# The first tile of a fused RWKV and feed-forward block: one difference for the shares, other mixings, a second norm without its mean

## The chip, the cores and the metric

The kernel runs on one core of one Trainium2 chip. The metric is the device time of one execution in microseconds (us); a profile of one such execution shows every instruction with its engine: PE (TensorE matmul), PEld (its weight loads), DVE (VectorE), ACT (ScalarE), POOL (GpSimd) and SP (SyncE, here only a DMA queue).

## The reference

Input x has 2 sequences of 4096 steps with 256 features, all in float32. The block is x + attention(norm(x)), then x + feed-forward(norm(x)). The norm has no scale or offset.

```python
def _layernorm(x, axis=-1, eps=1e-05):
    m = jnp.mean(x, axis=axis, keepdims=True)
    v = jnp.var(x, axis=axis, keepdims=True)
    return (x - m) / jnp.sqrt(v + eps)

# attention: x_prev is x one step earlier, zero at the start of a sequence
xk = x * time_mix_k + x_prev * (1.0 - time_mix_k)      # likewise xv, xr
k = jnp.einsum('btd,ed->bte', xk, W_k)                 # likewise v, and r through a sigmoid
# one step of the recurrence, p and q its state:
new_p = jnp.maximum(p, u + k_t)
scale_old = jnp.exp(jnp.maximum(p - new_p, NEG_CLAMP))
scale_cur = jnp.exp(jnp.maximum(u + k_t - new_p, NEG_CLAMP))
wkv_t = (scale_old * q + scale_cur * v_t) / (scale_old + scale_cur + EPS)
new_p2 = jnp.maximum(p + w, k_t)
q2 = jnp.exp(jnp.maximum(p + w - new_p2, NEG_CLAMP)) * q + jnp.exp(jnp.maximum(k_t - new_p2, NEG_CLAMP)) * v_t
# output: einsum of r * wkv with W_o

# feed-forward, with ternary weights and a scale for each output
h = jax.nn.silu(_tlin(x, w1_w, w1_s)) * _tlin(x, w2_w, w2_s)
h = jax.nn.gelu(_tlin(h, h1_w, h1_s), approximate=False)
h = jax.nn.gelu(_tlin(h, h2_w, h2_s), approximate=False)
return _tlin(h, w3_w, w3_s)
```

The two weights of `wkv_t` are a sigmoid of the difference u + k - p and of its negative; the kernel computes them so, and calls them shares.

## The kernel before

Features lie on the 128 partitions, in two heads (halves of the 256 features, index `h` or `c`); time lies along the free axis in 16 tiles of `TS` = 512 steps, of which 8 make a sequence. `halves` are the two halves of a tile in time. The feed-forward products run on TensorE in a rounded type, each value as a high and a low part (`split_product`, L186 and L187; `split`, L193 and L194). The attention products, the means and the norms of the first tile are full float32.

From the second tile on, the attention of tile i + 1 (`attention`, with `wkv` for a head) and the first norm of tile i + 2 (`normalise`, through `layernorm` and `total`) are generators whose pieces are placed between the pieces of the feed-forward of tile i (`ffn`); the loop at the end of `split_block` says at which step of `ffn` a piece is emitted. Their sums over features go to GpSimd as an all-reduce over the partitions (L207, with the sum of the two heads before it at L205).

The first tile has nothing to hide behind, so `first_tile` is written out by hand: every operation of it goes through `on` (line 358 in the profile, whatever the operation), which queues it behind the last one on the same engine. An operation can be emitted inside `behind(engine)` or `in_turn()`. Both rest on `tc.issue_after(ins)`, which orders only the instructions of the block that are on the engine of `ins`, behind `ins` in that engine's queue; it adds no wait between engines. Where such an order is missing, the scheduler may issue an instruction as soon as it thinks it ready, as it does with the copies of the carried state in `wkv` (L252, L253).

In order, the first tile does this. The means come from products with a constant matrix (`mean_w`). `first_layernorm` subtracts them, squares on ACT, adds the squares of the two heads on DVE, sums them over the features with one-column products (`var`), takes the root on ACT and the reciprocal on DVE, spreads it over the partitions with products (`rstd`) and multiplies. `keep_warm` fills PE's waits with products that nobody reads (`unread`).

The token mixing is folded into the weights of key and value (`scale`, tiles `ws`: a weight scaled by the mix and by its complement, the second applied to x one step earlier), which makes 4 products for each head; for the receptance the mixed input is built on ACT and added on GpSimd (tiles `mx`), which makes 2. `keys` are projected first, head 0 in two halves; then the values `v`, then the receptances `r`.

`differences` scans the running maximum (`lm`) and takes two differences for each head: key against the decayed state, into `sc`, and key plus `u` against the state, into `so`. `scales` makes the decay factors with Exp, two sigmoids make the shares, `state` scans the numerator (`num`), `result` multiplies and adds, and `y` is the result times r. Then come the output products (`ps_o`), the residual add into `x_sb`, again means and norm, and the rounding into `x2_hi` and `x2_lo`, with which the feed-forward of the first tile begins (`pa`, `pb`).

`load_table` evaluates a function on one column into `root` ahead of its need, so that ACT loads its table early; a small all-reduce on `root` does the same for GpSimd.

Of the kernel before, what the change touches and what calls it, by code (L numbers as in the profile page):

```python
# [9 lines left out]
F32 = mybir.dt.float32  # L10
# [56 lines left out]
def split_block(ctx, tc, flags, x, vecs, w_attn, w1, w2, h1, h2, w3, out):  # L67
# [35 lines left out]
    small = const.tile([P, 2], F32, name="small")  # L103
# [4 lines left out]
    for m, queue in enumerate((nc.scalar, nc.sync, nc.sync)):  # L108
        queue.dma_start(out=wa_sb[:, m], in_=w_attn[:, m])
# [31 lines left out]
    vector.tensor_scalar(unmix, vec[:, 0 : 3 * ND], -1.0, 1.0, ALU.mult, ALU.add)  # L141

# [59 lines left out]
    def total(a, b, tag):  # L202

        both = one.tile([P, TS], F32, tag=tag, name="both")
        marks["both"] = vector.tensor_tensor(both, a, b, ALU.add)  # L205
        everywhere = one.tile([P, TS], F32, tag="total", name="total")
        marks["sum"] = nc.gpsimd.partition_all_reduce(everywhere, both, channels=P, reduce_op=ReduceOp.add)  # L207
        return everywhere

    def layernorm(src, new_xc, tag, spread=False):  # L210


        mean = total(src[:, 0, :], src[:, 1, :], tag)
# [24 lines left out]
    def wkv(h, k, v, r, y, first):  # L238
# [9 lines left out]
        if first:  # L248
            vector.memset(lm[:, 0:1], LOG_ZERO)
            vector.memset(num[:, 0:1], 0.0)  # L250
        else:
            vector.tensor_copy(lm[:, 0:1], log_max[:, h : h + 1])  # L252
            vector.tensor_copy(num[:, 0:1], numer[:, h : h + 1])  # L253
# [33 lines left out]
    def normalise(i):  # L287
# [15 lines left out]
        yield from layernorm(x_sb, new_xn, "rstd1", spread=True)  # L303
# [3 lines left out]
    def attention(i):  # L307

        first = tiles[i][1] == 0
# [16 lines left out]
        for h in range(ND):  # L326
# [8 lines left out]
            yield from wkv(h, *kvr, y, first)  # L335
# [44 lines left out]
    def first_layernorm(src, xc, means):  # L380
# [4 lines left out]
        for mean, p in zip(means, halves):  # L385
            for h in range(ND):
                add(xc[:, h, p], src[:, h, p], mean, ALU.subtract)
            activation(sq[:, :, p], xc[:, :, p], AF.Square)
        varis = []
        for p in halves:  # L390
            add(sq[:, 0, p], sq[:, 0, p], sq[:, 1, p])
            var = ps_ffn.tile([P, TS // 2 // P], F32, tag="pf", name="var")
            for b in range(TS // 2 // P):
                t = slice(p.start + b * P, p.start + (b + 1) * P)
                matmul(var[:, b : b + 1], sq[:, 0, t], mean_w[:, 0:1], start=True, stop=True)
# [14 lines left out]
        for rstd, p in zip(spread, halves):  # L410
            for h in range(ND):
                add(xc[:, h, p], xc[:, h, p], rstd, ALU.mult)
            yield

    def first_tile(second):

        x_sb = loaded.pop(0)
        xn = wide.tile([P, ND, TS], F32, tag="wide", name="xn0")
# [23 lines left out]
        norm = first_layernorm(x_sb, xn, means)  # L442
# [3 lines left out]
        scaled = [[hid.tile([P, ND, D], F32, tag=tag, name="ws") for tag in ("hi", "lo")] for m in range(2)]  # L446
# [5 lines left out]

        next(norm)
# [8 lines left out]
        keep_warm(unread, 3, 2 * P)  # L462
        scale(0, (1, 1), (0, 1))
        scale(1, (0, 0), (1, 0), (1, 1), (0, 1))
# [3 lines left out]
        mx, then = (wide.tile([P, ND, TS], F32, tag="wide", name="mx") for _ in range(2))  # L468
        for c in range(ND):
            j = 2 * ND + c  # L470
            activation(mx[:, c, :], xn[:, c, :], AF.Copy, scale=vec[:, j : j + 1])
            activation(then[:, c, 1:], xn[:, c, : TS - 1], AF.Copy, scale=unmix[:, j : j + 1])
            on("gpsimd", "tensor_tensor", mx[:, c, 1:], mx[:, c, 1:], then[:, c, 1:], ALU.add)
        load_table(AF.Exp)
        on("gpsimd", "tensor_copy", prev, xn[:, :, TS - 1 :])

        on("gpsimd", "partition_all_reduce", root, eps, channels=P, reduce_op=ReduceOp.add)

        def project(m, h, kind, p=whole):
# [3 lines left out]
            if m == 2:  # L483
                for c in range(ND):
                    matmul(ps, wa_sb[:, 2, c, block], mx[:, c, :], start=c == 0, stop=c == ND - 1)
# [3 lines left out]
            shifted = slice(p.start + skip - 1, p.stop - 1)  # L489
            matmul(ps, now[:, 0, :], xn[:, 0, p], start=True, stop=False)  # L490
# [6 lines left out]
        keys = [[(project(0, 0, attn, p), p) for p in halves], [(project(0, 1, attn), whole)]]  # L497
        v = [project(1, h, ffn) for h in range(ND)]
        r = [project(2, h, ffn) for h in range(ND)]

        def differences(h):
            w, u = col(DECAY, h), col(FIRST, h)
            for k, p in keys[h]:
                t, after = lm[h][:, p], lm[h][:, p.start + 1 : p.stop + 1]
# [3 lines left out]
                on("vector", "scalar_tensor_tensor", so[h][1][:, p], k, u, t, ALU.add, ALU.subtract)  # L508
            on("vector", "tensor_scalar", sc[h][0], sc[h][1], NEG_CLAMP, 0.0, ALU.max, ALU.min)
            on("gpsimd", "tensor_copy", log_max[:, h : h + 1], lm[h][:, TS:])  # L510

        def scales(h):
            activation(sc[h][0], sc[h][0], AF.Exp)
            activation(sc[h][1], sc[h][1], AF.Relu)
            activation(sc[h][1], sc[h][1], AF.Exp, scale=-1.0)


        def state(h):
            on("vector", "scalar_tensor_tensor", sc[h][1], sc[h][1], MIN_SCALE, v[h], ALU.max, ALU.mult)
            on("vector", "tensor_tensor_scan", num[h][:, 1:], sc[h][0], sc[h][1], num[h][:, 0:1], ALU.mult, ALU.add)  # L520
# [440 lines left out]
```

## Time and profile before

| | us |
|---|---|
| median of 3 runs | 1541.54 (1541.45 to 1542.15) |
| the profiled execution, own time | 1540.95 |
| span of its instructions | 1539.4 |
| first feed-forward product starts | 39.16 |
| PE busy up to there | 36.61 |
| PE busy over the span | 1529.8 |

The profile has a page (busy times, chain of work that ended last, groups of instructions) and answers to questions on the trace (chain in order of time, timeline by engine, busy time in given stretches). Times count from the start of the span. In a line of the timeline stand start, length, engine, line, operation, the tiles written and read, and in brackets the idle time of the engine before it and what ended that. In a line of the windows stand the stretch and its length, then the busy time and the number of instructions of PE, PEld, DVE, ACT and POOL, then the granted clock of PE, the share of the DMA engines and GB/s. A float32 product shows as two records.

### The profile page before, as it was taken

The page shows a single profiled execution, that of the slowest core. Times are in us where ns is not written, and L with a number is a line of the kernel's source. Part 1 is how long each engine was busy: PE and PEld are TensorE (multiplying, and loading weights), DVE is VectorE, ACT ScalarE, POOL GpSimd, SP SyncE. Part 2 cuts the span into 40 slices and gives each one's busy share as a digit, 9 for nine tenths or more (in the row PEclk, how much of TensorE's full clock was granted, in tenths as well). Part 3 has the DMA queues.
Part 4 walks back from the last instruction along what each step waited for, and adds up shares of the span by engine and source line. Part 5 has one row for each costly group of instructions (what it writes and reads, how often), then busy time and mean ns, then how long its engine had stood idle before and what let it go on. Part 6 is the DMA issues. An engine that isn't in the chain of part 4 may idle for free.

```text
span 1539.4 us, 16523 instructions
## 1 busy us (share of the span) xinstructions
PE 1529.8 (99%) x6260; PEld 1172.8 (76%) x6260; DVE 1069.8 (69%) x1598; ACT 1047.3 (68%) x1348; POOL 240.5 (16%) x118
## 2 busy tenths in 40 slices
PE   9999999999999999999999999999999999999998
PEld 6778787777877778777787777877777787777886
DVE  7886676866768677785777768677686777855531
ACT  6685957759587595866858668595775858656542
POOL 4131021110211101112011121101111021100100
PEclk9999999999999999999999999999999999999999
DMA  7612030220302103031130311203122030210302
GB/s 274 137 55 89 14 118 33 82 69 14 134 18 96 55 26 133 7 110 42 45 113 14 117 35 59 93 10 120 35 77 74 14 130 21 96 41 28 117 9 83
DMA packets 39702, 109.16 MB, mean 71 GB/s; under 512 B 3712, under 2 KB 12672, under 8 KB 39104
## 3 DMA queue, kind: packets, MB, share of 16 engines
q1 hardware_dynamic: 25760, 79.86, 15.8%
q0 software_dynamic: 13296, 27.53, 5.7%
q8 instruction: 51, 0.84, 0.2%
q10 hardware_dynamic: 560, 0.66, 0.1%
q14 instruction: 35, 0.29, 0.1%
HBM read 99.64 MB, written 12.58 MB: 73 GB/s over the span
## 4 chain that ended last, share of the span: by engine, by line
PE 98%; DVE 1%; ACT 1%; issue 0%; DVEq 0%; ACTq 0%
PE ph L186 30%; PE ph L187 30%; PE pa L186 4%; PE pb L186 4%; PE po L187 4%; PE po L186 4%; PE pa L187 4%; PE pb L187 4%; PE ps_k L179 3%; PE ps_o L179 3%; PE ps_r L179 3%; PE ps_v L179 3%; PE ps_k L358 0%; PE unread L358 0%; DVE scale L358 0%; PE ps_v L358 0%
## 5 line engine op out<-in xcount | busy, mean ns | idle before, releaser
L186 PE MATMUL ph<-hi,h_sb 128*128 128x512 f32 x2048 | 815.7, 399 | 0.2 <-ACT hi L193 0.2
L187 PE MATMUL ph<-lo,h_sb 128*128 128x512 f32 x2048 | 811.5, 397 | 0.0
L186 PEld LDWEIGHTS ph<-hi,h_sb 128*128 128x128 f32 x2048 | 384.6, 188 | 98.5 <-issue 18.2
L187 PEld LDWEIGHTS ph<-lo,h_sb 128*128 128x128 f32 x2048 | 384.5, 188 | 96.9 <-issue 15.3
L207 POOL PARTITION_ALL_REDUCE total<-both x60 | 205.1, 3419 | 857.6 <-DVE both L205 442.7
L615 DVE TENSOR_TENSOR lo<-full,hi 128x512 fp32r<-128x512 f32 x256 | 197.2, 773 | 140.0 <-ACT full L614 137.1
L612 ACT ACTIVATE hi<-ph,vec 128x512 fp32r<-128x512 f32 x256 | 175.6, 686 | 125.7 <-PE ph L187 124.6
L596 ACT ACTIVATE gated<-pa,vec 128x512 f32<-128x512 f32 x128 | 87.4, 683 | 139.0 <-PE pa L187 137.2
L614 ACT ACTIVATE full<-ph,vec 128x512 f32<-128x512 f32 x256 | 175.3, 685 | 0.3
L597 DVE SCALAR_TENSOR_TENSOR gated<-pb,vec,gated 128x512 f32<-128x512 f32 x128 | 95.9, 749 | 70.9 <-PE pb L187 66.6
L612 ACT ACT_TABLE_LOAD x103 | 132.1, 1283 | 1.8
L231 DVE RECIPROCAL rstd<-rstd 128x256 f32<-128x256 f32 x60 | 102.8, 1731 | 2.1 <-ACT rstd L227 2.1
L193 ACT ACTIVATE hi<-gated 128x512 fp32r<-128x512 f32 x128 | 80.4, 628 | 33.8 <-DVE gated L597 33.5
L186 PE MATMUL pa<-x_hi,w_sb 128*128 128x512 f32 x256 | 101.9, 398 | 0.1
L186 PE MATMUL pb<-x_hi,w_sb 128*128 128x512 f32 x256 | 101.8, 398 | 0.0
L187 PE MATMUL pb<-x_lo,w_sb 128*128 128x512 f32 x256 | 100.5, 392 | 0.0
L187 PE MATMUL pa<-x_lo,w_sb 128*128 128x512 f32 x256 | 100.4, 392 | 0.0
L194 DVE TENSOR_TENSOR lo<-gated,hi 128x512 fp32r<-128x512 f32 x128 | 96.3, 760 | 4.8
L187 PE MATMUL po<-lo,w_sb 128*128 128x512 f32 x256 | 99.6, 389 | 0.0
L186 PE MATMUL po<-hi,w_sb 128*128 128x512 f32 x256 | 99.6, 389 | 0.0
L621 DVE SCALAR_TENSOR_TENSOR x_sb<-po,vec,x_sb 128x512 f32<-128x512 f32 x32 | 24.0, 751 | 72.1 <-PE po L187 72.1
L262 DVE TENSOR_TENSOR_SCAN lm<-vec,lm,ps_k 128x512 f32<-128x512 f32 x30 | 38.4, 1279 | 40.7 <-PE ps_k L179 40.7
(145 smaller groups left out, 1741.3 us busy)
## 6 DMA issues: line engine op xcount, KB each, us to landing
h_sb<-h_hbm SPq DMA_DIRECT2D x128, 512.0 KB, 3.2
raw<-in_h SPq DMA_DIRECT2D x32, 256.0 KB, 2.7
x_sb<-in_x POOLq DMA_DIRECT2D x15, 512.0 KB, 4.1
out<-x_sb POOLq DMA_DIRECT2D x15, 512.0 KB, 3.2
h_sb<-in_h POOLq DMA_DIRECT2D x1, 4096.0 KB, 18.7
h_hbm<-in_h POOLq DMA_DIRECT2D x8, 512.0 KB, 8.6
w_sb<-in_w POOLq DMA_DIRECT2D x3, 1024.0 KB, 9.6
raw<-in_w SPq DMA_DIRECT2D x12, 256.0 KB, 2.5
```

The lines of the kernel that those rows point to most:

```text
L179: tensor.matmul(psum, weights(c), src[c], start=c == 0, stop=c == n - 1)
L186: tensor.matmul(psum, weights(c), hi, start=c == 0, stop=False)
L187: tensor.matmul(psum, weights(c), lo, start=False, stop=c == n - 1)
L193: marks["rounded"] = scalar.activation(hi, full, AF.Copy)
L194: marks["rest"] = vector.tensor_tensor(lo, full, hi.bitcast(F32), ALU.subtract)
L207: marks["sum"] = nc.gpsimd.partition_all_reduce(everywhere, both, channels=P, reduce_op=ReduceOp.add)
L231: vector.reciprocal(rstd[:, p], rstd[:, p])
L596: scalar.activation(full, pa, AF.Silu, scale=col(S1, f))
L597: vector.scalar_tensor_tensor(full, pb, col(S2, f), full, ALU.mult, ALU.mult)
L612: scalar.activation(hi, ps, AF.Gelu, scale=col(scales, f))
L614: marks["rounded"] = scalar.activation(full, ps, AF.Gelu, scale=col(scales, f))
L615: marks["rest"] = vector.tensor_tensor(lo, full, hi.bitcast(F32), ALU.subtract)
```

## The change

Only the first tile's code, the first two steps that depend on it, and one list of steps change.

- The weights of value are not scaled any more: ACT and GpSimd build its mixed input for both heads, and value takes 2 products for each head. For receptance, head 1 of the input goes through scaled weights and head 0 through a mixed input (`mxr`), 3 products for each head. The loads of the two weights change places.
- The keys of both heads are projected in halves. One difference is kept for each head; the shares are sigmoids of it with a bias (`offset`: decay plus first, and its negative). Both heads' exponentials come before both heads' shares, and both states before both results.
- The rows of the output weights are centred (`centred`: minus their mean over the outputs) on DVE, and the second norm works on the centred x plus the output by these weights, with no mean taken. The output by the plain weights (`gain`) is projected too, and added to `x_sb` for the residual at the end. In that norm the squares of the two heads are added by the `var` products.
- The sum of the two heads of tile 2's x (`summed`) is made on GpSimd in the first tile; copies into `root` make GpSimd wait for DVE; the copies of carried state to GpSimd come after `y`.
- In the second tile the copies of the carried state are queued with `in_turn`. The first block of `ffn` of the first tile takes all high parts before the low ones. During `ffn` of the first tile the first norm of the third tile is emitted one step later.

```diff
-    for m, queue in enumerate((nc.scalar, nc.sync, nc.sync)):
+    for m, queue in ((0, nc.scalar), (2, nc.sync), (1, nc.sync)):
...
+    offset = small[:, 2:].rearrange("p (a b) -> p a b", a=2)
+    vector.tensor_tensor(offset[:, 0, :], vec[:, DECAY : DECAY + ND], vec[:, FIRST : FIRST + ND], ALU.add)
+    vector.tensor_scalar(offset[:, 1, :], offset[:, 0, :], -1.0, None, ALU.mult)
...
-            vector.tensor_copy(lm[:, 0:1], log_max[:, h : h + 1])
-            vector.tensor_copy(num[:, 0:1], numer[:, h : h + 1])
+            with in_turn() if i == 1 else nullcontext():
+                vector.tensor_copy(lm[:, 0:1], log_max[:, h : h + 1])
+                vector.tensor_copy(num[:, 0:1], numer[:, h : h + 1])
...
-    def first_layernorm(src, xc, means):
+    def first_layernorm(xc, out, centre):
...
-            add(sq[:, 0, p], sq[:, 0, p], sq[:, 1, p])
+            centre(xc, sq, p)
+        yield
+        for p in halves:
             var = ps_ffn.tile([P, TS // 2 // P], F32, tag="pf", name="var")
+            chunks = range(1 if xc is not out else ND)
+            if xc is not out:
+                add(sq[:, 0, p], sq[:, 0, p], sq[:, 1, p])
             for b in range(TS // 2 // P):
                 t = slice(p.start + b * P, p.start + (b + 1) * P)
-                matmul(var[:, b : b + 1], sq[:, 0, t], mean_w[:, 0:1], start=True, stop=True)
+                for c in chunks:
+                    matmul(
+                        var[:, b : b + 1], sq[:, c, t], mean_w[:, 0:1], start=c == 0, stop=c == chunks[-1]
+                    )
...
+        with behind("vector"):
+            on("gpsimd", "tensor_tensor", summed, loaded[1][:, 0, :], loaded[1][:, 1, :], ALU.add)
         scale(0, (1, 1), (0, 1))
-        scale(1, (0, 0), (1, 0), (1, 1), (0, 1))
+        scale(2, (0, 1), (1, 1))
...
+        mxr, thenr = (hid.tile([P, TS], F32, tag=tag, name="mxr") for tag in ("hi", "lo"))
+        for m, c, mixed, step in ((1, 0, mx[:, 0, :], then[:, 0, :]), (1, 1, mx[:, 1, :], then[:, 1, :]), (2, 0, mxr, thenr)):
+            j = m * ND + c
+            activation(mixed, xn[:, c, :], AF.Copy, scale=vec[:, j : j + 1])
+            activation(step[:, 1:], xn[:, c, : TS - 1], AF.Copy, scale=unmix[:, j : j + 1])
+            if m == 1:
+                on("gpsimd", "tensor_tensor", mixed[:, 1:], mixed[:, 1:], step[:, 1:], ALU.add)
...
+        def rest_of_gpsimd():
+            on("gpsimd", "tensor_copy", root, sc[0][0][:, 0:1])
+            on("gpsimd", "tensor_tensor", mxr[:, 1:], mxr[:, 1:], thenr[:, 1:], ALU.add)
+            on("gpsimd", "tensor_copy", prev, xn[:, :, TS - 1 :])
+
+            on("gpsimd", "partition_all_reduce", root, eps, channels=P, reduce_op=ReduceOp.add)
+
+
+        centred = hid.tile([P, ND, D], F32, tag="hi", name="centred")
+        row = tmp.tile([P, ND], F32, tag="each", name="row")
         for c in range(ND):
...
+            on("vector", "tensor_reduce", row[:, c : c + 1], wa_sb[:, 3, c, :], mybir.AxisListType.X, ALU.add)
+        on("vector", "tensor_scalar", row, row, 1.0 / D, None, ALU.mult)
+
+        def centre(c):
+            on("vector", "tensor_scalar", centred[:, c, :], wa_sb[:, 3, c, :], row[:, c : c + 1], None, ALU.subtract)
+
+        centre(0)
...
+            if m == 2:
+                matmul(ps, now[:, 1, :], xn[:, 1, :], start=True, stop=False)
+                matmul(ps[:, 1:], then[:, 1, :], xn[:, 1, shifted], start=False, stop=False)
+                matmul(ps, wa_sb[:, m, 0, block], mxr, start=False, stop=True)
+                return ps
...
-        keys = [[(project(0, 0, attn, p), p) for p in halves], [(project(0, 1, attn), whole)]]
+        keys = [[(project(0, h, attn, p), p) for p in halves] for h in range(ND)]
         v = [project(1, h, ffn) for h in range(ND)]
-        r = [project(2, h, ffn) for h in range(ND)]
...
-                on("vector", "scalar_tensor_tensor", so[h][1][:, p], k, u, t, ALU.add, ALU.subtract)
...
         def scales(h):
+            activation(so[h][0], sc[h][1], AF.Relu)
+            activation(so[h][0], so[h][0], AF.Exp, scale=-1.0)
             activation(sc[h][0], sc[h][0], AF.Exp)
...
+        def shares(h):
+            activation(so[h][1], sc[h][1], AF.Sigmoid, bias=offset[:, 1, h : h + 1])
+            activation(sc[h][1], sc[h][1], AF.Sigmoid, bias=offset[:, 0, h : h + 1], scale=-1.0)
...
+        differences(0)
+        rest_of_gpsimd()
+        r = [project(2, h, ffn) for h in range(ND)]
+        scales(0)
+        differences(1, lambda: centre(1))
+        scales(1)
+        for h in range(ND):
+            shares(h)
         for h in range(ND):
             activation(r[h], r[h], AF.Sigmoid)
         load_table(AF.Sqrt)
         y = wide.tile([P, ND, TS], F32, tag="wide", name="y")
         state(0)
+        state(1)
         result(0)
-        state(1)
...
+        for h in range(ND):
+            on("gpsimd", "tensor_copy", log_max[:, h : h + 1], lm[h][:, TS:])
+            on("gpsimd", "tensor_copy", numer[:, h : h + 1], num[h][:, TS:])
+
+        on("gpsimd", "tensor_copy", root, y[:, 1, TS - 1 :])
+        with behind("vector"), behind("scalar"), behind("gpsimd"):
             next(second)
...
+        gain = [ps_sum.tile([P, TS], F32, tag="ps", name="gain"), ps_attn.tile([P, TS], F32, tag="pa", name="gain")]
+
+        def output(h, c, p=whole):
+            matmul(gain[h][:, p], wa_sb[:, 3, c, h * P : (h + 1) * P], y[:, c, p], start=c == 0, stop=c == ND - 1 and p.stop == TS)
+
         for c in range(ND):
             for ps_of, p in zip(banks, halves):
                 for h in range(ND):
-                    matmul(ps_of[h], wa_sb[:, 3, c, h * P : (h + 1) * P], y[:, c, p], start=c == 0, stop=c == ND - 1)
...
+                    matmul(ps_of[h], centred[:, c, h * P : (h + 1) * P], y[:, c, p], start=c == 0, stop=c == ND - 1)
+        output(0, 0)
+
+        def plus_output(x2, sq, p):
             for h in range(ND):
...
+                add(x2[:, h, p], xc[:, h, p], banks[p.start * 2 // TS][h])
+                activation(sq[:, h, p], x2[:, h, p], AF.Square)
...
+        norm = first_layernorm(x2, x2, plus_output)
+        next(norm)
+        for p in halves:
+            next(norm)
+            output(0, 1, p)
+        for _ in range(2):
+            next(norm)
+        for c in range(ND):
+            output(1, c)
+        run(norm)
...
+        activation(x2_hi[:, :, halves[0]], x2[:, :, halves[0]], AF.Copy)
+        for h in range(ND):
+            activation(x2_hi[:, h, halves[1]], x2[:, h, halves[1]], AF.Copy)
+            add(x2_lo[:, h, :], x2[:, h, :], x2_hi[:, h, :].bitcast(F32), ALU.subtract)
+        for h in range(ND):
+            add(x_sb[:, h, :], x_sb[:, h, :], gain[h])
...
-            if step in ((NH - 3, NH, NH + 3, NH + 4, NH + 5) if i > 0 else (NH + 2, NH + 5, NH + 7, NH + 8, NH + 9)):
+            if step in ((NH - 3, NH, NH + 3, NH + 4, NH + 5) if i > 0 else (NH + 3, NH + 6, NH + 8, NH + 9, NH + 10)):
```

## The prediction

> **What bounds the kernel now.** I read the page first: its busy times, then its chain of work.
>
> ```profile
> PE 1529.8 (99%) x6260; PEld 1172.8 (76%) x6260; DVE 1069.8 (69%) x1598; ACT 1047.3 (68%) x1348; POOL 240.5 (16%) x118
> ...
> PE 98%; DVE 1%; ACT 1%; issue 0%; DVEq 0%; ACTq 0%
> ```
>
> PE is the bound on the whole, so only what moves PE's work counts. The windows say where PE has room.
>
> ```profile
> 0.00:39.16 39.16, 36.61 (x147) 24.58 (x147) 28.04 (x67) 25.96 (x44) 17.08 (x29) 1.00 0.79 275
> 39.16:70.00 30.84, 30.62 (x122) 22.76 (x123) 26.62 (x36) 19.13 (x26) 4.03 (x3) 1.00 0.74 164
> 70.00:135.50 65.50, 65.50 (x270) 50.43 (x269) 52.72 (x76) 47.29 (x59) 14.10 (x5) 1.00 0.21 69
> 230.00:1500.00 1270.00, 1270.00 (x5195) 975.90 (x5194) 887.15 (x1310) 877.48 (x1121) 189.66 (x77) 1.00 0.19 63
> ```
>
> From 39.16 us, the first product of the first feed-forward (`pa`), PE is full but for 0.22 us, and the change leaves the products behind that point as they are. So the change is worth what it moves that first `pa`, and nothing else unless a new wait appears later. Third came the chain of waits up to there, in order of time (start, length).
>
> ```profile
> 10.54 6.88 PE ps_k L358 x24
> 17.42 3.44 PE ps_v L358 x8
> ...
> 20.96 0.70 DVE scale L358
> ...
> 29.62 0.43 DVE y L358
> ...
> 30.09 2.00 PE ps_o L358 x8
> 32.09 1.74 PE mean L358 x8
> ...
> 35.30 0.44 DVE sq L358
> ...
> 38.48 0.64 ACT x_hi L358
> 39.16 0.50 PE pa L186
> ```
>
> Three stretches: keys and the first value on PE to 20.96, one run of DVE from 20.96 to `y` at 29.62, and output, second norm and rounding from 30.05 to 39.16. Last the timeline by engine, for what GpSimd does beside DVE.
>
> ```profile
> 7.61 0.43 DVE L358 TENSOR_TENSOR sq<-sq 128x256 f32<-128x256 f32 x1 [0.24 <-ACT sq L358]
> ...
> 12.83 2.51 POOL L358 TENSOR_TENSOR mx<-mx 128x511 f32<-128x511 f32 x2 [7.85 <-ACT mx L358]
> ...
> 23.68 0.40 POOL L358 PARTITION_ALL_REDUCE small<-small  x1 [8.21 <-ACT scale L358]
> ```
>
> **The change part by part.** Times are those of the profiled execution (span 1539.40, its own time 1540.95, 0.59 below the median 1541.54). Up to the keys' first product at 10.37 the old work is the same: the centred x goes to another buffer at the same price, and the two small `offset` operations (0.17 each, by the `unmix` row) fall into DVE's 0.37 us of idle before 5.50.
>
> *Value.* Its weights are no longer scaled twice; ACT builds the mixed input and GpSimd adds it, so each head takes 2 products instead of 4. A 128x512 product here is two records at 0.43 apart (ps_v, 8 records in 3.44). Value head 0 ends at 17.25 + 4 x 0.43 = 18.97, and DVE can use it 0.27 later, as before (20.69 to 20.96): 19.24, a gain of 1.72. Cover: ACT does 2 scalings fewer (0.45 each) and 2 mixings more (0.61 each); the value's are first, done at about 13.2, and GpSimd's two adds (1.28 each) end at 14.5, 2.7 before PE comes to them.
>
> *Receptance* now takes 3 products a head, 6 records each: 20.69 to 23.27 and 25.85, its sigmoids at 24.9 and 26.7, before DVE wants them (25.1, 27.7). `y` takes the buffer of the normed x, which receptance still reads to 24.99; with the 0.27 that is 25.26, so `y` of head 0 waits about 0.2.
>
> *One difference.* DVE loses one operation per head (two of 0.48, one of 0.75) and head 1 comes in halves as head 0 does. Its second half is ready at 17.46 as before; scan 0.75, difference 0.48, clamp 0.42 give 19.17 instead of 20.52, just under the 19.24. ACT then goes Exp, Exp, Sigmoid in one order: three table loads of 1.28 (17.88, 20.49, 23.61) become one. Exponentials of head 1 end at 20.6, the four shares at 22.5, 23.1, 23.7 and 24.3; DVE wants the first at 23.1. None of it is late.
>
> *DVE's run.* The same operations, with both states ahead of the results: from 19.24 by the old spacings (0.72, 1.20, 0.72, 1.20, 0.60, 0.72, 0.70 and so on), plus the 0.2, `y` of head 1 starts at 27.9 instead of 29.62. The two copies at 29.43 that go behind the feed-forward's operations save 0.1 and are in this. Gain so far 1.73.
>
> *Centred output weights* cost DVE two row sums, a tiny scaling and a subtraction ahead of the first scan. The trace has no reduction; nearest is the 128x256 add, 0.42, far end the 128x256 scan, 0.75. By 0.42 all takes 1.25 of 1.32 us idle. By 0.75 the first scan is 0.7 late, but a half now costs DVE 1.2 for PE's 1.72, so two halves win it back. Taken: 0.
>
> *Second norm.* From the end of `y`'s first half to `pa` it was 30.05 to 39.16, 9.11. Removed: mean products, their subtraction, two adds of squares, warm-up products. New, counted from 28.32: output products to 30.08 (8 x 0.215), then the plain output head 0 on PE to 30.94; meanwhile four adds onto the centred x (to 30.75) and four squares of 0.45. Eight var records instead of four double 0.52 to 1.04: var 0 by 31.98, half an output product 0.43, var 1 by 33.45, 0.43 again, then rstd 0 at 33.88. Multiplications of half 0 end at 35.34 (before: 36.25 to 37.7), half 1 at 36.04, rounding at 36.45 and 36.82. PE has the last two output products to 36.67: `pa` at about 36.7. That is 8.35, a gain of 0.76; the warm-up is replaced by real products and no gap on PE exceeds 0.8.
>
> *After `pa`.* The residual adds (2 x 0.69) lie before the first gated product. The first block takes high parts first, as many products. The third tile's norm moves with all it issues, two all-reduces on GpSimd, Square and Sqrt on ACT, their table loads; PE's sum is 65.50 of 65.50 in that stretch, so cost 0, bounds 0.4 either way (the one stall there is 0.22 and a slow start).
>
> *The early sum of tile 2* (`summed`) leaves DVE at 30.29, where 0.69 lay beside PE's output: at most 0.1. It goes to GpSimd. The order written around it names VectorE's queue and holds no GpSimd instruction, so it runs when tile 2's x is there: issued at 1.30, the slower of two transfers took 5.9, so about 7.2, to 8.5. DVE's add of squares starts at 7.61, both inputs in SBUF. What such a pair does is seen later:
>
> ```profile
> 48.55 3.22 POOL L207 PARTITION_ALL_REDUCE total<-both  x1 [8.58 <-DVE both L205]
> ...
> 49.10 2.22 DVE L194 TENSOR_TENSOR lo<-gated,hi 128x512 fp32r<-128x512 f32 x1
> 51.24 0.74 DVE L597 SCALAR_TENSOR_TENSOR gated<-pb,vec,gated 128x512 f32<-128x512 f32 x1
> 51.91 0.68 DVE L194 TENSOR_TENSOR lo<-gated,hi 128x512 fp32r<-128x512 f32 x1
> ```
>
> An add of 0.68 took 2.22 beside GpSimd. With no GpSimd add beside a DVE add of that kind in the trace, the bounds are 0 and 1.28 (a GpSimd add whole). I take the square add to end 0.75 to 1.0 late; reciprocal, var, rstd and the keys stand behind it in their queues, so everything after moves by about 0.75.
>
> The Trainium skill (SBUF — State Buffer, "Who interferes with whom") has a rule for it: a VectorE instruction with two SBUF inputs and a GpSimd instruction that reads SBUF exclude each other, and the later one waits for the whole of the earlier. By the rule alone the loss would be about 0.95 and the sum -1.55.
>
> Sum: -1.73 - 0.76 = -2.5, plus 0.75 for the collision: -1.75. Profiled execution 1539.2, median **1539.8**.
>
> **Rivals.** *No collision* (x of tile 2 lands later, or the two share): -2.5, 1539.0. For it: GpSimd's adds at 12.83 to 15.34 did not stretch the DVE operations beside them (0.75, 0.48), though those read one operand from PSUM. *More gain*: besides no collision, the slow start at 57.2 (0.5) goes and PE's last output products are not what `pa` waits for (0.27): -3.27, 1538.3. *More collisions*: the subtractions that centre the weights meet GpSimd's mixing adds; head 1's has only 0.3 of slack before its scan and the first can be held 1.28, part of which is won back: 0.8 more, 1540.7. *Slower*: GpSimd's small all-reduce on `root`. It started 8.21 after the copy before it, and GpSimd stood idle. Now a copy that waits for DVE and another add come ahead of it, so that its 8.2 begin at 17.4 to 18.2 and it ends at 26.0 to 26.8. ScalarE writes `root` after it with the Sqrt preload at about 28, and the squares stand behind that. It decides once the gap passes 10.2; if it were taken twice (16.4), the squares start at 35.2 for 30.2, 5.0 lost against 1.75 won: 1544.8. Against it: the old gap ended with an ACT operation (23.59), so part of it may have been a plain wait.
>
> The same skill (GPSIMD Engine Reference, "Instruction dispatch") says that a freshly loaded kernel pays about 6 us at its first call; a rate of 6 would end it by 24.6 and keep it hidden.
>
> **How the numbers follow.** Collision 0.48, no collision 0.22, more collisions 0.08, more gain 0.12, slower 0.10. About what a measurement of this kernel can tell from no change is 0.2%, 3.1 us: only 1538.3 is beyond it below, only 1544.8 above. So faster 0.12, same 0.78, slower 0.10. The range takes all cases but the slower one, with 0.7 of uncertainty above 1540.7: 1538.2 to 1541.4.
>
> **What would show it.** The first `pa` at 37.4 (36.7 without collision); first key product near 11.1 with a square add of about 1.3 us, or at 10.4 with 0.43; value head 0 done 1.7 earlier relative to the first key product; `y` head 1 8.65 after that; 8.4 from `y` to `pa`; PE without a new wait from there on. Wrong it is if `pa` comes before 36.0 or after 39, if PE shows a wait of over 0.5 us between `pa` and 135 us, or if DVE waits for ACT's shares or ACT for GpSimd.

## Result and profile after

The changed kernel takes 1545.36 us (median of 18 runs, 1543.97 to 1546.5) against 1541.57 (18 runs, 1541.01 to 1542.15) for the kernel before on the same chip: ratio 1.0024, 95% interval 1.0016 to 1.0031. It is slower by 3.8 us, where 1539.8 was forecast with 1541.4 as the upper end. The profiled execution took 1546.5 with a span of 1544.7, at a mean granted clock of 0.997. Fifteen of the 18 executions, at 0.998 or 0.999, took 1543.97 to 1545.81, so its profile shows about a microsecond more than a usual run loses.

The page gives the first sign: PE's busy time is the same to 0.4 us, the span is 5.3 longer, and the chain that ended last has lost 3% of the span from PE.

```profile
PE 1530.2 (99%) x6264; PEld 1173.5 (76%) x6264; DVE 1069.0 (69%) x1599; ACT 1046.6 (68%) x1350; POOL 246.3 (16%) x122
...
PE 95%; DVE 3%; ACT 1%; POOL 1%; DMA 0%; issue 0%; POOLq 0%; DVEq 0%
```

The windows, with the limits used for before (columns: length, busy time and count of PE, PEld, DVE, ACT and POOL, granted clock, DMA share, GB/s), put the loss in two stages. Between 39.16 and 70 PE now idles 1.11 us (before 0.22), between 70 and 135.5 it idles 3.27 (before 0), and there the clock's mean is 0.99.

```profile
39.16:70.00 30.84, 29.73 (x122) 22.26 (x121) 26.86 (x40) 20.26 (x28) 5.26 (x4) 1.00 0.90 195
70.00:135.50 65.50, 62.23 (x247) 46.38 (x246) 50.99 (x74) 45.67 (x56) 15.02 (x4) 0.99 0.20 69
```

The waits of PE name three that before had not (it had one of 0.2 behind the first `pa`):

```profile
PE po L191 <- DVE lo L689: 2.0, 2, 1.9
...
PE ps_o L183 <- DVE y L288: 1.3, 1, 1.3
PE ph L190 <- ACT hi L197: 1.1, 1, 1.1
```

To see what each costs I use the *lead*: the start of the n-th weight load of the first feed-forward in the profile before, less that of the same load after. It is positive where the changed kernel is ahead. Operations of the attention of tile 2 lie between these loads in another order in the two kernels, so it is read where the same ones are done in both. One profile stands against one other here, and x lands at another time in each: the first product of the keys starts at 10.37 in the profile before, and at 10.74 to 11.30 in the three other profiles of the same first tile (e8, e11, e4).

| place | before | after | lead | what lies between |
|---|---|---|---|---|
| first `pa` | 39.15 | 37.38 | +1.77 | the first tile, and x landing 0.32 later |
| 24th load of the first hidden layer | 59.72 | 59.05 | +0.67 | wait for `hi`, 1.1 |
| half-way through the second hidden layer | 111.81 | 112.75 | -0.95 | wait for `y`, 1.3, and changed order |
| last low part in `po` | 129.94 | 133.56 | -3.62 | waits for `lo`, 2.0 |
| second gate layer | 141.25 | 146.34 | -5.09 | 3.4 us at half clock |

**The first tile did about what was forecast.** The chain of waits up to `pa`, in order of time:

```profile
7.92 1.30 DVE sq L363
...
11.58 3.46 PE ps_k L363 x16
...
29.16 0.43 DVE y L363
...
36.02 1.72 PE gain L363 x4
37.74 0.47 PE pa L666 x2
```

`y` of head 1 starts at 29.16 (before 29.62), and `pa` comes 8.2 us behind it (before 9.5). From the first add of squares to `pa`, which leaves out when x lands, it is 30.1 us (before 32.2). What follows is about the other four rows of the table.

### The profile page after: what moved, and what is told of

It is laid out like the page before. It is cut to its first block, busy times and chain, and to the rows that moved or that the text cites. A ratio compares the mean times of both kernels' runs of the same rounds, so it can differ in the third digit from the quotient of the medians.

```text
span 1544.7 us, 16546 instructions
## 1 busy us (share of the span) xinstructions
PE 1530.2 (99%) x6264; PEld 1173.5 (76%) x6264; DVE 1069.0 (69%) x1599; ACT 1046.6 (68%) x1350; POOL 246.3 (16%) x122
## 4 chain that ended last, share of the span: by engine, by line
PE 95%; DVE 3%; ACT 1%; POOL 1%; DMA 0%; issue 0%; POOLq 0%; DVEq 0%
PE ph L190 29%; PE ph L191 29%; PE pa L191 4%; PE po L191 4%; PE pb L191 4%; PE po L190 4%; PE pa L190 4%; PE pb L190 4%; PE ps_k L183 3%; PE ps_r L183 3%; PE ps_v L183 3%; PE ps_o L183 3%; POOL total L212 1%; DVE rstd L236 0%; ACT scale L363 0%; DVE scale L363 0%
```

## The experiments

In all twelve runs the profile of before is the one shown above, and times are medians; the runs stand in the order of the questions. The kernel before, timed beside them, took 1541.53 to 1541.57; e9 to e12 ran on another chip than e1 to e8, and the kernel before takes the same on both.

**Which edit behind the first tile costs the time?** The change has two: the second tile's copies of the carried state are put in turn, and the third tile's norm comes a step later. The first four runs take them back on the new first tile, one, the other and both, and add both to the old first tile. Of the copies only those of head 1 are set free: those of head 0 stay in turn in every run on the new first tile.

```diff
 e1_steps_back, on the changed kernel:
-            if step in (... else (NH + 3, NH + 6, NH + 8, NH + 9, NH + 10)):
+            if step in (... else (NH + 2, NH + 5, NH + 7, NH + 8, NH + 9)):
 e2_head1_free, on the changed kernel:
-            with in_turn() if i == 1 else nullcontext():
+            with in_turn() if i == 1 and h == 0 else nullcontext():
 e3_both_back: both.
 e4_old_tile_both_edits: the kernel before, with the copies of the second
 tile in turn and the later steps.
```

> The changed kernel with the third tile's norm at its old steps again; the copies of the carried state stay in turn. Theory A (the copies of head 1, queued behind a low part that waits for ScalarE, delay the second tile's attention by 6 us, and all else follows): the wait for y near 103 us stays (over 1 us), y of head 1 stays after 103 us, and the time stays within 1 us of the changed kernel's 1545.4, or wins at most the 2 us of the wait for the last low part. Theory B (the norm one step later pushes the mixing of the third tile into the end of the feed-forward): the wait of 2.25 us for the last low part and the slow clock after it go, and the time falls to about 1542. Theory C (the earlier start itself upsets the order, neither edit alone): 1544 to 1546, with both waits.

> The changed kernel with the copies of the carried state in turn for head 0 only; the third tile's norm stays one step later. Theory A: scan of head 1 back to 82 to 84 us, y of head 1 at about 97 us, no wait for y; time about 1541 to 1542. Theory B: the wait for y goes too, but the wait for the last low part near 131 us stays at over 1 us, and the time is 1543 to 1544. Theory C: 1544 to 1546.

> Both edits undone: copies in turn for head 0 only, third tile's norm at its old steps, the new first tile kept. Theories A and B: no wait on TensorE between 60 and 135 us; what is left against the old kernel is the start at 37.4 us instead of 39.16 (1.8 won) and the wait at the end of the first layer, where the last Silu stands behind the Sqrt (1.1 lost): 1540.6 to 1541.2. Theory C: still 1543 or more.

> The old kernel with those two edits alone: copies of the carried state of the second tile in turn for both heads, third tile's norm one step later. Theories A and B: the same waits for y and for the last low part as in the changed kernel, with the first product at 39.16: 1543 to 1546. Theory C: as the old kernel, 1541.3 to 1542.

Two more complete the old tile's side, each edit alone on the kernel before:

> The old kernel with the copies of the second tile's carried state in turn for both heads, and nothing else. Theory A: scan of head 1 moves from 83.7 to about 90 us, a wait for y near 100 us and for a last low part near 131 us follow: 1543 to 1547. If in turn is harmful only with the earlier start: 1541.3 to 1542.

> The kernel before, with the third tile's norm a step later and nothing else. Theory: the later steps alone put the third tile's Sqrt and mixing ahead of the last low parts; a wait of 1.2 to 1.8 before a `po` product, no wait for `y`, time 1543.0 to 1543.6. Rival: it takes the copies in turn as well, which delay that norm by about 5 us; alone the steps cost under 0.4: 1541.4 to 1541.9, no wait for `lo`.

| first tile | neither edit | copies in turn | later steps | both |
|---|---|---|---|---|
| old | 1541.57 | 1541.76 (e8) | 1544.33 (e11) | 1544.21 (e4) |
| new | 1542.34 (e3) | 1548.45 (e1) | 1542.89 (e2) | 1545.36 |

| kernel | ratio to before | 95% interval |
|---|---|---|
| e8, old tile, copies in turn | 1.0002 | 0.9992 to 1.0011 |
| e11, old tile, later steps | 1.0020 | 1.0011 to 1.0029 |
| e4, old tile, both | 1.0016 | 1.0007 to 1.0026 |
| e3, new tile, neither | 1.0003 | 0.9993 to 1.0013 |
| e1, new tile, copies in turn | 1.0043 | 1.0027 to 1.0060 |
| e2, new tile, later steps | 1.0009 | 1.0000 to 1.0019 |

Against what was expected: e4 took the time of theories A and B (1544.21), with shorter waits, 0.5 for `y` and 1.4 for `lo`. e2 kept the wait for `lo` (1.8) as theory B had it, and comes 0.1 under its time. For e8 the rival was right, and the theory that the copies alone cost 2 us or more was wrong. For e11 the theory was right in the wait (1.9) and too low in the time (1544.33 for 1543.6 at most). For e1 and e3 no theory was right: e1 became 3.1 us slower, which none had, and e3 has no wait over 0.3 between 60 and 135 us, as A and B had it, but not their time.

So the costs don't add: the later steps cost 2.8 on the old tile, 0.6 on the new one with the copies free, and win 3.1 there with the copies in turn. The traces say why. Four times answer for each kernel: when the scan of head 1 starts, when `y` of head 1 does, when GpSimd begins the fourth all-reduce of the stretch, and when the last `lo` runs. Two norms share this stretch, the third tile's first (`xn`) and the second tile's second (`x2`, in the rows `x`), each with an all-reduce for the mean and one for the variance; the fourth is the variance of the second tile's second norm, since it reads the squares of `x` and the rounding of `x` into `x_hi` comes behind it.

| kernel | scan | `y` | all-reduce | last `lo` | wait for `y` | wait for `lo` |
|---|---|---|---|---|---|---|
| before | 83.67 | 97.82 | 112.68 | 128.27 | 0 | 0 |
| e3 | 84.25 | 98.30 | 114.26 | 127.34 | 0 | 0 |
| e8 | 90.01 | 102.01 | 116.12 | 129.20 | 0 | 0 |
| e11 | 83.12 | 99.26 | 117.24 | 132.30 | 0 | 1.9 |
| e4 | 90.61 | 102.81 | 117.68 | 132.74 | 0.5 | 1.4 |
| e2 | 83.96 | 98.89 | 117.25 | 130.87 | 0 | 1.8 |
| after | 90.24 | 104.03 | 117.28 | 132.82 | 1.3 | 2.0 |
| e1 | 91.37 | 105.18 | 122.17 | 135.25 | 1.3 | 2.5 |

*The copies.* In every kernel that has them in turn the scan starts 6 to 7.5 us later than in the same kernel without. The timeline of DVE after (in brackets the idle time before an operation and what ended it) shows what they stand behind: a low part that waits 5.04 us for ScalarE. Before, the scan ran ahead of a low part:

```profile
83.67 1.27 DVE L262 TENSOR_TENSOR_SCAN lm<-vec,lm,ps_k 128x512 f32<-128x512 f32 x1
84.86 1.54 DVE L615 TENSOR_TENSOR lo<-full,hi 128x512 fp32r<-128x512 f32 x1
```

After:

```profile
89.39 0.69 DVE L689 TENSOR_TENSOR lo<-full,hi 128x512 fp32r<-128x512 f32 x1 [5.04 <-ACT full L688]
89.99 0.15 DVE L258 COPY lm<-log_max 128x1 f32<-128x1 f32 x1
...
90.24 1.28 DVE L268 TENSOR_TENSOR_SCAN lm<-vec,lm,ps_k 128x512 f32<-128x512 f32 x1
```

The scan reads a column that a copy writes, and behind it is all of head 1 up to `y` and the third tile's norm. DVE idles 5 us; with the copy free (e2) the scan runs in that hole. On the old tile `y` is 4.2 us late and PE shows no wait for it (e8 costs 0.2 in all): in that profile PE comes to the products that read it at 102.77, just after `y` ends at 102.70. On the new tile `y` is 5.1 us later than in e2 and PE waits 1.3.

*The later steps.* They put the fourth all-reduce at 117.2 in e11 and e2, and the copies in turn alone put it at 116.1 (e8) or 122.2 (e1). In e11 the variance of the third tile's norm is reduced at 103.81 (before 94.99), so that the second tile's two all-reduces come at 107.89 and 117.24 (before 104.62 and 112.68). And on DVE the sum of squares that the last one reads, whose squares end at 113.55, stands behind the third tile's reciprocal and its multiplication:

```profile
115.78 0.69 DVE L235 TENSOR_TENSOR xn<-xn,rstd 128x512 f32<-128x512 f32 x1
116.38 0.69 DVE L205 TENSOR_TENSOR both<-sq 128x512 f32<-128x512 f32 x1
```

In e1 it is the sum for the second tile's mean that stands behind them, at 113.90 (after: 109.06). Of these eight kernels, PE waits for no `lo` where the fourth all-reduce begins at 116.1 or before, and waits where it begins at 117.2 or later; but its start alone doesn't decide, for in e10 below it begins at 115.96 and PE waits 0.8. In the changed kernel ScalarE holds the Sqrt of the second tile's second norm, which waits for it:

```profile
116.97 1.28 ACT L232 ACT_TABLE_LOAD   x1
122.05 0.73 ACT L232 ACTIVATE rstd<-total,small 128x512 f32<-128x512 f32 x1 [3.80 <-POOL total L212]
```

Two pairs of `hi` and `full` of the feed-forward stand behind that Sqrt, and the low parts need them. The rest of the delay is on DVE. Before, the last low part waited for ScalarE alone:

```profile
128.27 0.69 DVE L615 TENSOR_TENSOR lo<-full,hi 128x512 fp32r<-128x512 f32 x1 [1.85 <-ACT full L614]
```

After, the chain of waits shows DVE as the path up to the product that PE waits for:

```profile
127.92 0.60 DVE lo L689
128.52 0.66 DVE mx L324
129.18 1.14 DVE x_lo L198
130.32 0.60 DVE lo L689
130.92 0.66 DVE mx L324
131.59 1.32 DVE move L324 x2
132.91 0.61 DVE lo L689
...
133.56 0.50 PE po L191
134.06 0.42 PE po L190
```

One `mx` stands ahead of the last low part but one, and one `mx` and two `move` ahead of the last: the third tile's mixing, whose first product starts at 157.70. The last `lo` needs 131.31, where ScalarE's last `full` ends, and runs at 132.82. The second PE line shows the half clock too: 0.42 for a product, 0.43 in those behind it, 0.23 later.

**Is it the mixing?** Only the value's and receptance's mixing of the later tile is ordered behind the last `lo`; on DVE nothing else changes place in this stretch.

```diff
 e9_mixing_after_lo, on the changed kernel:
-                marks["rest"] = vector.tensor_tensor(lo, full, ...)
+                marks["rest"] = marks[i, layer] = vector.tensor_tensor(lo, full, ...)
...
+                with tc.issue_after(marks[0, 1].ins) if i == 2 and m else nullcontext():
                     vector.scalar_tensor_tensor(mx[:, h, :], move[:, h, :], ...)
```

> The changed kernel whole, with one edit: of the third tile's mixing, the four operations of value and receptance are ordered behind the last low part (`lo`) of the first feed-forward. Theory: TensorE's last wait, 2.25 us before a `po` product, is partly these operations standing ahead of that `lo` on VectorE: its input was ready at 131.31, it ran at 132.82. So the wait shrinks to about 0.8, the stretch at half clock behind it (1.47 lost) goes with it, and the time is 1542.5; 1544.0 if the half clock stays. Rival: the mixing only fills time in which `lo` waits for ScalarE anyhow; then the wait stays above 1.8 and the time at 1545.4. Nothing before 120 us changes in either (wait for `y` 1.3, for `hi` 1.1).

The theory was right. It takes 1542.55 (ratio 1.0008 [0.9999, 1.0017]): 2.8 less than the change by the medians, from the place of four operations. The waits of PE in its profile: 0.4 for `lo`, the other two as they were; the granted clock is 1.00 throughout this stretch.

```profile
PE ps_o L183 <- DVE y L288: 1.3, 1, 1.3
PE ph L190 <- ACT hi L197: 1.1, 1, 1.1
...
PE po L191 <- DVE lo L689: 0.4, 1, 0.4
```

The lead lost at this place falls from 2.67 (-0.95 to -3.62) to 1.20 (-0.42 to -1.62), by 1.47. The two profiles differ by 3.58 at the second gate layer: this 1.47, about as much for the half clock, and 0.51 for an earlier `pa` (36.87), since the add of squares met no sum of GpSimd's there (0.43). How the 2.8 of the medians divides is not shown.

**What is the wait for `hi`?** With both edits back (e3), the first tile hands over 2.55 us ahead in the profile, an execution of 1541.09, and the median is still 1542.34. The profile after shows on ScalarE, near the end of the gate layer:

```profile
53.53 1.28 ACT L232 ACT_TABLE_LOAD   x1
54.83 0.72 ACT L232 ACTIVATE rstd<-total,small 128x512 f32<-128x512 f32 x1
55.57 1.28 ACT L670 ACT_TABLE_LOAD   x1
56.87 0.69 ACT L670 ACTIVATE gated<-pa,vec 128x512 f32<-128x512 f32 x1
```

The root of the second tile's norm comes between two `gated`, with two table loads around it. Before, it came behind the last `gated`:

```profile
53.94 0.69 ACT L596 ACTIVATE gated<-pa,vec 128x512 f32<-128x512 f32 x1
...
56.48 0.72 ACT L227 ACTIVATE rstd<-total,small 128x512 f32<-128x512 f32 x1
```

The list of steps for that norm was not edited, and yet its root now falls elsewhere among the `gated`. e5 moves it one step on:

```diff
 e5_silu_before_sqrt, on e3:
-                if step in (0, NH - 2, NH - 1):
+                if step in (0, NH - 1):
```

> The kernel of e3 (new first tile, both edits undone) with the root of the second tile's first norm emitted after the last Silu instead of before it. If the 1.50 us between two products near 57 us is the Sqrt and the reload of the Silu table ahead of the last gate, it goes to at most 0.6, ScalarE has one table load less, and the time falls by about 1 us from 1542.3 to 1541.3. If that wait only moves (the root is then late for the mixing of the second tile), the time stays at 1542.3.

1540.61 (ratio 0.9995 [0.9985, 1.0005]): 1.73 won by the medians, where about 1 was expected. The times of e3 fall into two groups (three of 1540.94 to 1541.09, seven of 1541.90 to 1542.55), and so do those of e5 (five of 1540.02 to 1540.32, five of 1540.89 to 1541.52); between like groups it is 0.7 to 1.2, about the wait of 1.1, and the rest of the 1.73 is how many fell into which. In its profile the last `gated` is at 52.81, the table load at 54.98, and no wait for `hi` is left. That the earlier start made the scheduler change the order is argued from the traces, not tried by itself: the wait of 1.1 is there in all six profiles of the new first tile with that list of steps (after, e1, e2, e3, e6, e9), and in none of the old one.

**The sum on GpSimd.** In the first tile it may meet the add of squares on DVE. In the timeline after it started first, and the add is the longer for it; in that of e12 the add started first:

```profile
7.66 1.27 POOL L363 TENSOR_TENSOR both<-x_sb 128x512 f32<-128x512 f32 x1 [2.67 <-DMA x_sb<-in_x]
...
7.92 1.28 DVE L363 TENSOR_TENSOR sq<-sq 128x256 f32<-128x256 f32 x1 [0.23 <-ACT sq L363]
```

```profile
8.43 0.42 DVE L363 TENSOR_TENSOR sq<-sq 128x256 f32<-128x256 f32 x1 [0.36 <-ACT sq L363]
...
8.53 1.47 POOL L363 TENSOR_TENSOR both<-x_sb 128x512 f32<-128x512 f32 x1 [3.55 <-DMA x_sb<-in_x]
```

The one that starts second pays: 0.85 for DVE, 0.20 for GpSimd. Of the eight profiles with the sum at this place it starts first in two (after and e1, where the add takes 1.28 and 1.51), and second or behind the add in six. e6 and e7 emit the sum after the norm, behind a copy that waits for its last multiplication, so that the two can't meet; e7 also has e5's order, and steps between the old and the new ones. e12 is e7 with the sum where the change has it.

```diff
 e6_sum_after_norm, on e3:
-        with behind("vector"):
-            on("gpsimd", "tensor_tensor", summed, loaded[1][:, 0, :], ...)
...
         run(norm)
+        on("gpsimd", "tensor_copy", root, xn[:, 1, TS - 1 :])
+        on("gpsimd", "tensor_tensor", summed, loaded[1][:, 0, :], ...)
 e7_all_mended: e5, e6, and the list (NH + 3, NH + 5, NH + 7, NH + 8, NH + 9)
 e12_middle_steps_silu: e7 without e6's edit
```

> The kernel of e3 with the early sum of tile 2 on GpSimd behind a copy that waits for the last multiplication of the first norm. If that sum collides with the add of squares whenever x of tile 2 lands ahead of it, the second add of squares takes 0.43 and the first feed-forward product comes at 36.6 in every run; in e3 1540.9 and 1542.4 are then the runs without and with a collision, and the time falls to 1541 to 1541.6 with less scatter. If the scatter comes from elsewhere (between 70 and 105 us), the times are as those of e3.

> The new first tile with copies in turn for head 0 only, the third tile's first sum at the later step and the rest of its norm at the old steps, the last Silu ahead of the root, and the early sum after the norm. If the first tile is worth 2.5 us and the waits behind it come from these orders alone, no wait on TensorE over 0.4 us is left between 37 and 135 us, and the time is 1538.6 to 1539.5. If the earlier start is lost again to other waits, 1541 or more.

> As the run with all mended, but GpSimd's sum of the second tile back where the change has it (beside the square add). If the later sum is what that run lost against the one with Silu first (1541.07 against 1540.61), this gives 1540.4 to 1540.7; if the middle steps (NH + 3, NH + 5, ...) are, 1541.0 to 1541.3.

e6: 1542.24, against 1542.34 of e3. e7: 1541.07. e12: 1540.25 (ratio 0.9993 [0.9984, 1.0002]). So e6 and e7 missed the forecast times, and e12 came 0.15 below the range that it had for the later sum as the cause. The later sum wins nothing, and e12 is 0.8 faster without it than e7. In e6 the add of squares takes 0.42, but from the first key product to `y` of head 1 it is 18.47 us against 17.70 in e3: GpSimd's two mixing adds, now behind the sum, start at 13.18, just ahead of the subtraction on DVE that centres the first output weights. It takes 1.32, in e3 0.35, and PE waits 0.8 more for `y`.

```profile
13.29 1.32 DVE L363 TENSOR_SCALAR centred<-wa_sb,row 128x256 f32<-128x256 f32 x1
```

What the sum avoids in one place it costs in another. The scatter did shrink, as e6 expected (its ten times lie within 0.74, those of e3 within 1.61), but about the upper group of e3. The middle steps cost nothing, and win 0.4 against e5, which is within the spread of both.

**All together, another way.** e10 keeps the change's later steps and mends the rest: head 1's copies free, e5's order, e9's mixing.

> The changed kernel with its later steps, and three mends: head 1's state copies free again, Silu ahead of the Sqrt of the second tile's norm, the third tile's value and receptance mixing behind the last `lo`. If the three costs are apart from each other: 1542.9 (the run with head 1 free) less 1.7 (what the Silu order won) less 1.4 (the mixing): 1539.8, no wait of TensorE over 0.9. Rival: each mend moves the queues and the gains don't add; 1541 to 1542, with a wait that is none of the three.

1541.95 (ratio 1.0004 [0.9995, 1.0013]): the rival was right in the time, since the gains of the three edits don't add, but not in the wait: the one that is left, for `lo`, is one of the three. The 1.7 that it counts for the Silu order is the difference of e3's and e5's medians. Its lead is 2.10 half-way through the second hidden layer, more than in any other run, and 0.33 after `po`. The mixing is out of the way, but the Sqrt still waits 3.04 us for the all-reduce, and PE waits 0.8 for `lo` and 0.3 for `hi`. That part belongs to the later steps, and none of the three mends reaches it.

The best kernel is e12: the new first tile, head 1's copies free, the middle steps, Silu ahead of the root. It is 1.3 us below before by the medians; the interval of the ratio just reaches one. Of the 2.12 us that its first tile hands over in the profile, 0.95 is left at the second gate layer, with no wait of PE over 0.4 on the way; the products of the second tile's attention lie in another order there, and what takes the rest stays open.

## Why the prediction was wrong

*Right: the first tile, its total partly by luck.* `pa` was forecast at 37.4 with the collision and 36.7 without; it came at 37.38 after, and at 36.61 in e3's profile, which had none. But three misses cancel in the 37.38. x landed 0.32 later than before (first add of squares at 7.26 for 6.94), which is why the first key product came at 11.41 where 11.1 was forecast. From there to `y` of head 1 it took 17.75 (before 19.25): 1.50 won for 1.73. From `y` to `pa` it took 8.23 from the start of `y` (before 9.54): 1.31 won for 0.76. (The forecast of 8.4 counted from the end of the first half of `y`; from there 7.8 was measured.) Counted from the first add of squares, `pa` came 32.2 later in all four profiles of the old tile, 29.4 in the six of the new one without a collision and 30.1 and 30.3 in the two with it: the tile is worth 2.8 and about 2.0, where 2.5 and 1.75 were forecast. The square add with the collision: about 1.3 forecast, 1.28 measured; here the Trainium skill (SBUF — State Buffer, "Who interferes with whom") and the trace agree, and e12 shows its other half, that the order of issue decides who waits. The two row sums, bounded by 0.42 and 0.75 each, took 0.74 together. Two rivals didn't come. In that of more collisions, head 1's subtraction took 0.68 beside a GpSimd add and nothing was late; its price came only in e6, for the first subtraction. In the other, ScalarE waits for GpSimd's small all-reduce: this one was forecast to end at 26.0 to 26.8 and ended at 26.81, behind 7.71 us of idle, and nothing waited for it.

*Failed: "cost 0, bounds 0.4 either way" for the third tile's norm.* Alone it costs 2.76 (e11). The reason given was that PE is full in that stretch, 65.50 of 65.50. That shows that no wait is there before, not how far a feeder can be moved until one is. The room was in the trace: the last `lo` ended at 128.96, and the weights of the product that reads it were loaded at 129.94, 0.98 later. The move takes the third tile's last all-reduce from 94.99 to 103.81, and with it the last one of the second tile's second norm from 112.68 to 117.24, 4.6 us. The text listed all that moves with the norm, and stopped short of asking what then stands behind it: the second tile's second norm on DVE and GpSimd, two pairs of activations behind the Sqrt of that norm, and the last low parts behind the mixing. Beside the copies in turn the same move wins 3.1 (e1): there the old steps put the third tile's pieces ahead of the sum for the second tile's mean.

*Failed: "save 0.1" for the copies.* I counted what the two copies take away from DVE and not who is queued behind them. In turn, they stand behind a low part that waits for ScalarE, and the scan of head 1 is held 6 us; freeing them gives 2.47 back (after against e2).

*Missing: the order on ScalarE.* The forecast took the work behind `pa` as a fixed block that shifts with its start. It isn't: the root of the second tile's norm fell ahead of the last `gated`, which took 1.1 of the 1.77 that the first tile had won, and about as much is got back by mending it (0.7 to 1.2 between like groups of e3 and e5).

So the stated mark of a wrong prediction, a wait of over 0.5 us of PE between `pa` and 135 us, was met three times. Most of the gain was spent before 60 us, and the rest is loss. How much of the median the half clock makes up stays open: the profile has it, and so by their mean clock of 0.997 have two more of the 18; for those at 0.998 and 0.999 that figure can't tell, since such a stretch takes about 0.001 off it.

## What to carry to other kernels

An engine that is full before the change has no spare room in it, but its feeders have a due time. For every step that is moved, or queued behind another, take from the trace the end of the feeder and the start of the product that needs it, and compare that slack with the length of the move, through all that queues behind the moved instruction on each engine. A start that comes earlier is a change of order too: where two activation tables share a stage, look at which comes first afterwards.

## What was not expected of the hardware

- After a gap of 2.25 us between two `po` products the granted clock was 0.5 for 3.41 us (0.43 for a product, 0.23 else), 1.47 us lost. In e11's profile the same gap, 130.78 to 133.03, left the clock at 1.00. The Trainium skill (TensorE: Matmul & The Clock Gate, "Why this matters for your kernels") asks for no gaps over about 3 us between products; here a shorter one was enough in one profile, and not in another. The traces say what differed. In the profile after, the stretches at one clock last 129.71, 3.41 and 1402.88 us, which are 38, 1 and 411 times 3.41; e1's, the other profile with a half clock here, has the same three. Counted on that grid, PE idled 2.01 us in the stretch just before the half clock (130.52 to 133.94) and 2.39 in e1. In e11 a limit of the grid at 132.80 cuts the gap, and the stretch with most idle time has 1.62; in e2 it has 1.44, in the other ten profiles at most 1.3.
- Beside a GpSimd all-reduce the same operation takes one or three times its time: `move` over 128x1024 took 1.22 in the profile after and 3.27 in e2's, `sc` over 128x512 0.41 in e12's and 1.45 in e3's.
